# Constant operand rows of the first batch loaded in two parts, the second behind the first operand loads

## The chip, the cores and the metric

The kernel runs on one core of a Trainium2 chip. The metric is the time of the whole program on the device, in microseconds (us). Five engines work beside each other, each through its own queue in order: PE (TensorE, matrix products), DVE (VectorE), ACT (ScalarE), POOL (GpSimd) and SP (SyncE, which here issues DMAs and computes nothing). ACT and POOL issue DMAs too. A DMA's data are moved by the core's 16 DMA engines.

## The reference, cut to what matters

Input is `x` of shape (8, 512, 128): 8 batches of 512 tokens. Four sublayers follow each other, each with a residual and a layer norm:

```python
x = _layernorm(x + _L0_attn_ref(x, ...))   # 16 heads of 8, with a linear distance bias
x = _layernorm(x + _L0_ffn_ref(x, ...))    # gated, blockwise FP4 quantisation
x = _layernorm(x + _L1_attn_ref(x, ...))   # 16 heads of 8, no bias
x = _layernorm(x + _L1_ffn_ref(x, ...))    # two layers of windowed attention and GEGLU
```

The change lies in the first one:

```python
slopes = jnp.power(2.0, 8.0 * jnp.arange(0, -H, -1) / H)
q, k, v = heads of (x @ W_qkv.T + b_qkv)
scores = jnp.einsum('bhqd,bhkd->bhqk', q, k) / math.sqrt(Hd)
rel = jnp.abs(pos[None, :] - pos[:, None])
probs = jax.nn.softmax(scores - slopes * rel, axis=-1)
out = (probs @ v, heads joined) @ W_out.T + b_out
```

## The kernel before, in words

**Operands.** For one batch, the operand tiles `qs_[i]` and `ks_[i]` (i is the batch's parity) have 128 partitions, 8 pairs of heads and 512 tokens. The partitions are two halves of 64, j = 0 and 1, one for each head of a pair. Of a half, partitions 0 to 31 hold four groups of 8 rows: the head's 8 dimensions, split in a high and a low float32r part and put in the products that are wanted. Partitions 32 to 47 hold the constant rows `rowq` or `rowk`, the same for all pairs, from which the same matmul makes the greater part of the distance bias. Partition 63 holds -1 in `ks_` (row 16 of `rowk`) and, in `qs_`, the row maxima that are put there later. A scores matmul reads 63 or 64 partitions of one pair, so it needs the loaded rows and the constant rows of that pair.

**How the first batch gets there.** `constant_rows(0, held)` (line 1147, called in 1205) copies the constant rows from SBUF to SBUF, all 8 pairs, in six DMAs on SP: for each half one for row 63 of k, one for the 16 rows of q, one for the 16 rows of k. Then `attention` (line 252) is called. Its `plan` (line 392) makes the first batch's operands: `begin_x` transposes x, `begin_qk` (line 212) projects q, then k, lets POOL split them into `parts`, and writes these to DRAM (`far`, two DMAs each, one for each half). `load_qk` (line 232) reads them back in the order of rows that the tiles want, with eight DMAs of 8 partitions for each call:

```python
for part in (slice(0, 2), slice(2, 4), 1):
    load_qk(0, batch[0], 0, part, held)
    load_qk(0, batch[0], 1, part, held_a)
```

So pairs 0 and 1 come first, then 2 and 3, then 4 to 7; q on SP (`held`), k on ACT (`held_a`). Behind these on SP come, through `first_late` (line 1166), the constant rows of the second batch (`constant_rows(1, held)`), the x of batches 2 to 7 (`load_late`, line 103) and then the weights of the next sublayer.

**Steps.** Attention is a row of steps, 8 for each unit of two pairs (four units a batch). Step s of the scores takes pair `2 * g + i % 2` and the query block `i // 2`: steps 0 to 7 need pairs 0 and 1, steps 8 to 15 pairs 2 and 3, steps 16 to 31 pairs 4 to 7, and step 32 begins the second batch. In a step PE makes the scores of a block of 128 queries for both heads (`s_ps`), DVE takes their row maxima (`m`). PE's buffer `s_ps` is double. `LAG` = 16 steps later the same unit's transposed scores (`t_ps`) go through ACT's exponentials (`e`) to the product with v (`av`); `shift` (line 323) takes the maxima of a unit to row 63 of q with a POOL DMA. The second batch's operands are begun at steps 8 (`begin_x`), 10 and 12 (`begin_qk`).

**Order and waits.** Whatever goes through `held`, `held_a`, `Kept` or `keep_in_program_order` stays in the order of the program on its queue. The framework puts semaphore waits between tiles' writers and readers, by region. Its DMAs on SP and ACT share eight completion semaphores in turn, and a DMA is issued only when the one before it on the same semaphore has landed.

Of the kernel before, what the change touches and what calls it, by code (L numbers as in the profile page):

```python
# [9 lines left out]
F32 = mybir.dt.float32  # L10
# [9 lines left out]
B, S, D = 8, 512, 128  # L20
# [31 lines left out]
def body(ctx, tc, x, consts, rows, wa0, wa1, acols, bo, wf, wqkv, wo, w1, w2, cols, b2r, qs, ks, out):  # L52
# [26 lines left out]
    held, held_a = (lambda e: lambda **k: tc.keep_in_program_order(e.dma_start(**k)))(nc.sync), (  # L79
        lambda e: lambda **k: tc.keep_in_program_order(e.dma_start(**k))  # L80
    )(nc.scalar)
# [21 lines left out]
    def load_late():  # L103
        for b in range(2, B):
            held(out=xn[:, b * NT : (b + 1) * NT, :], in_=xv[:, b])
# [64 lines left out]
    def quantized_tokens(b, y, m, small):  # L170

        flat = lambda t: t[:, b * NT : (b + 1) * NT, :].rearrange("p c d -> p (c d)")
        return quantized(flat(xn), S, y, m, flat(xs), small)
# [75 lines left out]
        return begin_x, begin_qk, load_qk, begin_v  # L249


    def attention(li, alibi, qs_, ks_, va, batch, late=None, spare=None, alone=0):

# [4 lines left out]
        with ExitStack() as st:  # L260
# [9 lines left out]
            def with_bias(b):  # L270
                for c in range(NT):
                    pool_.tensor_tensor(xs[:, b * NT + c, :], xn[:, b * NT + c, :], crow, ALU.add)
# [119 lines left out]
            def plan():  # L392
                nonlocal work, crow
                const, work = pool("ac", 1), pool("aw", 2)
                dram = pool("ad", 2, space=bass.MemoryType.DRAM)
                begin_x, begin_qk, load_qk, begin_v = operand_steps(
                    li, qs_, ks_, va, mm, tr, bank, work, dram, qb[:, li : li + 1]
                )

                bvb = const.tile([P, P], F32, name="bvb")  # L400
                dve.tensor_copy(bvb, col[:, 3:4].broadcast_to([P, P]))
                crow = const.tile([P, P], F32, name="crow")
                nc.scalar.dma_start(out=crow, in_=bo[li].partition_broadcast(P))
                for n in range(B * G):
                    b, g = divmod(n, G)
                    s, z = n * NU, n * NU + LAG
                    later(z + 12, divide, units[n])
                    for blk in range(NT):
                        for part in range(2):
                            later(z + 2 * blk + 3 + part, values, units[n], blk, part)  # L410
                    if g == 0 and begun <= b + 1 < B:

                        early = max(s - 10, 8)
                        later(early, begin_x, b + 1, batch[b + 1])
                        later(early + 2, begin_qk, b + 1, batch[b + 1], 0)
                        later(early + 4, begin_qk, b + 1, batch[b + 1], 1)
                        for part in range(2):
                            for j in range(2):
                                later(max(s, 8) + 6 + 12 * part + 2 * j, load_qk, b + 1, batch[b + 1], j, part)
                        later(s + 20, begin_v, b + 1, batch[b + 1])  # L420
                        later(s + 20, with_bias, b + 1)
                    if g == 0:
                        later(s + 20 if b else alone, hold_o, batch[b])
                    if g == G - 1:
                        later(z + 15, end_o, batch[b])
                        later(z + 18, end_y, b, batch[b])
                if not begun:
                    begin_x(0, batch[0])
                    begin_qk(0, batch[0], 0, held)
                    begin_qk(0, batch[0], 1, held)  # L430
                    begin_v(0, batch[0])
                    for part in (slice(0, 2), slice(2, 4), 1):
                        load_qk(0, batch[0], 0, part, held)
                        load_qk(0, batch[0], 1, part, held_a)

                def bias_row():
                    ps = bank("c_ps")[:, 0:P]
                    mm(ps, lhsT=bvb, rhs=w[:, W_O : W_O + P], start=True, stop=True)
                    dve.tensor_tensor(crow, ps, crow, ALU.add)
                    for b in range(max(begun, 1)):  # L440
                        with_bias(b)

                later(alone + 4, bias_row)
                if late:
                    late()
                if spare:
                    spare(later, lambda b: (b * G + G - 1) * NU + LAG + 22, work, bank, mm, tr, p_s)

            for s in range(B * G * NU + LAG + 20):
                if s == alone:  # L450
                    plan()
                n, i = divmod(s, NU)
# [691 lines left out]

    with tc.tile_pool(name="ops", bufs=1) as ops:
        qs_, ks_ = ([at, ops.tile([P, 8, S], F32R, name=f"{n}1")] for n, at in (("q", q0), ("k", k0)))
        def constant_rows(i, start):
            for j in range(2):
                for t, at, src in ((ks_[i], 63, rowk[16:17]), (qs_[i], 32, rowq), (ks_[i], 32, rowk[0:16])):
                    n = src.shape[0]  # L1150
                    start(
                        out=t[64 * j + at : 64 * j + at + n].bitcast(F32),
                        in_=src.bitcast(F32).unsqueeze(1).broadcast_to([n, 8, S]),
                    )

        va = [va0, ops.tile([P, NT, 16, 32], F32, name="va1")]

        def filled(v):
            pool_.memset(v, 0.0)
            pool_.memset(v[:, :, :, 8:9], 1.0)  # L1160

        filled(va[0])
        wgu = ops.tile([P, 2, NI], F32, name="wgu")
        wd = ops.tile([P, 3, D], F32, name="wd")

        def first_late():
            dve.memset(qs_[1].bitcast(F32), 0.0)
            pool_.memset(ks_[1].bitcast(F32), 0.0)
            filled(va[1])
            constant_rows(1, held)  # L1170
            load_late()

        def first_spare(later, done, work, bank, mm, tr, p_s):
            temps = lambda: [work.tile([P, S], F32, tag=t, name=t, bufs=1) for t in ("qy", "qm")]
            later(64, load_weights)
            for j in range(3):
                quantize_weights(later, 28 + 11 * j, j, temps, work, bank, tr)

            def tokens(b):
                for i, f in zip((1, 4, 5, 6), quantized_tokens(b, *temps(), work)):  # L1180
                    later(done(b) + i, f)

            for b in range(B - 1):
                later(done(b), tokens, b)

            def turned():

                ps, h["xT"] = bank("xq_ps")[:, 0 : 2 * P], work.tile([P, S], F32, tag="qy", name="xqT", bufs=1)
                for t in range(2):
                    tr(ps[:, t * P : (t + 1) * P], xs[:, t, :], ident)  # L1190
                act_.copy(h["xT"][:, 0 : 2 * P], ps)

            def table():

                one = small.tile([P, 1], F32, tag="one", name="one", bufs=1)
                act_.activation(one, half[:, 0:1], AF.Silu)

            h, end = {}, done(B - 1) - 22 + 2 * NT
            later(end - 1, turned)
            later(end + 2, lambda: gates.append(gate(h["xT"], 0)))  # L1200
            later(end + 3, table)
            later(end + 5, lambda: gates.append(gate(h["xT"], 1)))

        second, gates = [], []
        constant_rows(0, held)
        psum = ExitStack()
        p_s, p_t, p_av = (
            psum.enter_context(tc.tile_pool(name=n, bufs=k, space=PSUM)) for n, k in (("as", 2), ("at", 3), ("aav", 1))
        )
        for _ in attention(0, True, qs_, ks_, va, [], first_late, first_spare):  # L1210
            pass
        nc.gpsimd.memset(rowq.bitcast(F32), 0.0)
        for i in range(2):
            for j in range(2):
                nc.sync.dma_start(
                    out=ks_[i][64 * j + 32 : 64 * j + 48].bitcast(F32),
                    in_=rowq.bitcast(F32).unsqueeze(1).broadcast_to([16, 8, S]),
                )
        last = ffn1()
        for _ in ffn0(qs_, ks_, va, second, gates, lambda: attention(1, False, qs_, ks_, va, second, spare=last[0], alone=16)):  # L1220
            pass
        psum.close()
# [98 lines left out]
```

## Time and profile before

| | us |
|---|---|
| median of 3 runs | 1742.46 |
| lowest and highest | 1741.09, 1747.34 |
| profiled execution, its own time | 1744.98 |
| span of the profiled execution | 1743.1 |
| PE busy in the span | 1637.8 (94%) |

The profile is one execution. Its times count from the start of the span. In its lists a line has the start, the length, the engine (a `q` behind it means the engine's queue, so an issue and no work of the engine), the operation and `out<-in` by the program's names; a length of several instructions (`x4`) goes from the first start to the last end. The length of a DMA in a queue is the time its issue took, not that of its data. In the chain of waits "DMA q<-far" is time until the landing of such a DMA. Waits are inferred from semaphore events. The granted clock is the share of full speed at which PE was let run.

### The profile page before, as it was taken

Reading aid. Unit: us, or ns where it says so; the run is one execution under the profiler, and the core shown is the slowest. Engines: PE = TensorE matmul, PEld = TensorE weight load, DVE = VectorE, ACT = ScalarE, POOL = GpSimd, SP = SyncE. Lnnn points to the kernel's source line nnn. Section 1 sums busy time; section 2 is a strip of 40 time slices with the busy share of each in tenths; the row PEclk is TensorE's granted clock in tenths of the full one; section 3 lists DMA queues with packets and bytes.
Section 4 is the critical chain, followed back from the end, with each engine's and each line's share of the span. In section 5 each row is a group of like instructions: output and inputs, shape, how many; then the busy total and the mean of one; then the engine's idle time right before and its main releaser. Section 6 shows DMA issues by size and latency. Waiting matters only on the chain.

```text
span 1743.1 us, 42097 instructions
## 1 busy us (share of the span) xinstructions
PE 1637.8 (94%) x16304; PEld 950.2 (55%) x16305; DVE 1381.6 (79%) x2209; ACT 1257.5 (72%) x2996; POOL 911.9 (52%) x974
## 2 busy tenths in 40 slices
PE   4999999999988789999999989999999999999995
PEld 2455555455546544444444446666766666666664
DVE  4688777878839888888888847788888888888873
ACT  1577777776764558878778867788887888888883
POOL 3223331332126741323222257888888888888873
PEclk7799999999999989999999999999999999999998
DMA  5735222321110234333323101111111111111110
GB/s 125 155 68 143 65 54 47 67 59 26 14 14 1 73 66 84 64 62 73 68 52 55 44 1 35 35 35 38 41 38 35 35 41 38 44 41 42 37 35 25
DMA packets 80777, 90.27 MB, mean 52 GB/s; under 512 B 46097, under 2 KB 58385, under 8 KB 76610
## 3 DMA queue, kind: packets, MB, share of 16 engines
q1 hardware_dynamic: 75504, 85.52, 23.2%
q8 instruction: 130, 2.13, 0.5%
q10 hardware_dynamic: 978, 1.52, 0.3%
q0 software_dynamic: 4096, 0.54, 0.3%
q14 instruction: 69, 0.57, 0.1%
HBM read 41.85 MB, written 18.87 MB: 35 GB/s over the span
## 4 chain that ended last, share of the span: by engine, by line
PE 77%; DVE 7%; ACT 6%; POOL 5%; issue 2%; DMA 2%; SPq 1%; DVEq 0%; POOLq 0%; ACTq 0%
PE av L258 15%; PE s_ps L258 12%; PE t_ps L258 9%; PE y_ps L645 5%; PE sp L645 4%; PE o_ps L645 3%; PE t_ps L645 3%; PE v_ps L645 3%; PE p_ps L645 2%; PE q_ps L645 2%; PE k_ps L645 2%; ACT e L48 2%; PE gp L645 2%; PE ap L645 2%; PE o_ps L259 2%
## 5 line engine op out<-in xcount | busy, mean ns | idle before, releaser
L48 DVE TENSOR_REDUCE m<-s_ps 128x2 f32<-128x1024 f32 x512 | 622.5, 1224 | 154.1 <-PE s_ps L258 148.9
L48 ACT ACTIVATE e<-t_ps 128x512 f32<-128x512 f32 x1024 | 556.3, 596 | 178.4 <-PE t_ps L258 170.1
L258 PE MATMUL av<-e,va 128*32 128x256 f32 x4096 | 328.1, 393 | 10.8 <-ACT avs L48 10.7
L258 PE MATMUL s_ps<-k,q 63*128 63x512 f32 x1024 | 265.3, 511 | 20.5 <-DMA q<-far 14.4
L48 POOL DMA_DIRECT2D q<-mt x128 | 68.9, 542 | 365.9 <-ACT mt L48 365.9
L258 PE MATMUL t_ps<-q,k 64*128 64x512 f32 x1024 | 248.1, 448 | 1.3 <-ACT e L48 1.3
L645 ACT ACTIVATE pw<-sp,m,was_v 128x128 f32<-128x128 f32 x512 | 227.6, 480 | 1.5 <-DVE m L645 1.0
L258 PEld LDWEIGHTS s_ps<-k,q 63*128 63x128 f32 x1024 | 99.8, 189 | 227.9 <-issue 151.3
L645 POOL TENSOR_TENSOR was_v<-was_v 128x16 f32<-128x16 f32 x64 | 187.6, 2931 | 5.3
L258 PEld LDWEIGHTS av<-e,va 128*32 128x32 f32 x4096 | 81.5, 108 | 100.5 <-issue 58.9
L258 PEld LDWEIGHTS t_ps<-q,k 64*128 64x128 f32 x1024 | 122.5, 189 | 22.7 <-ACT e L48 10.6
L645 POOL TENSOR_TENSOR pw<-pw,den 128x1024 f32<-128x1024 f32 x64 | 121.3, 1895 | 9.1 <-DVE den L645 9.1
L645 ACT ACTIVATION_READ_ACCUMULATOR pw<-sp,m,was_v 128x1 f32 x512 | 115.9, 226 | 0.0
L258 PEld LDWEIGHTS <-sel 64*128 64x128 bf16 x2048 | 67.3, 98 | 76.6 <-issue 53.3
L645 DVE TENSOR_REDUCE m<-sp 128x4 f32<-128x512 f32 x128 | 82.2, 683 | 21.9 <-PE sp L645 20.1
L48 POOL CAST parts<-x 128x512 fp32r<-128x512 f32 x32 | 19.5, 610 | 138.4 <-ACT x L48 138.4
L645 POOL TENSOR_TENSOR was_k<-was_k,was_q 128x512 f32<-128x512 f32 x64 | 88.0, 1376 | 6.1 <-DVE was_q L645 6.1
L645 ACT COPY v<-v_ps 128x512 f32<-128x512 f32 x64 | 37.6, 588 | 72.7 <-PE v_ps L645 72.7
L645 PEld LDWEIGHTS t_ps<-cst,was_k 128*128 128x128 f32 x512 | 59.7, 142 | 43.2 <-issue 22.4
L645 DVE COPY pT<-p_ps 128x512 f32<-128x512 f32 x128 | 79.8, 664 | 0.5 <-PE p_ps L645 0.5
L645 PEld LDWEIGHTS p_ps<-cst,pw 128*128 128x128 f32 x512 | 59.8, 141 | 33.0 <-issue 28.0
L645 DVE TENSOR_REDUCE was_v<-was_k 128x16 f32<-128x1024 f32 x64 | 77.0, 1204 | 0.0
(191 smaller groups left out, 3282.1 us busy)
## 6 DMA issues: line engine op xcount, KB each, us to landing
far<-parts SPq DMA_DIRECT2D x64, 256.0 KB
q<-far SPq DMA_DIRECT2D x248, 64.0 KB
k<-far SPq DMA_DIRECT2D x240, 64.0 KB
ve<-v SPq DMA_DIRECT2D x112, 128.0 KB
xn<-in_x SPq DMA_DIRECT2D x8, 256.0 KB
q<-mt POOLq DMA_DIRECT2D x128, 4.0 KB, 3.1
hn<-xs SPq DMA_DIRECT2D x16, 128.0 KB
hn<-xs SPq DMA_DIRECT2D x16, 112.0 KB
```

What stands on the lines that cost most here:

```text
L48: return lambda *a, **k: self.tc.keep_in_program_order(f(*a, **k))
L258: mm = lambda *a, **k: tc.keep_in_program_order(nc.tensor.matmul(*a, **k))
L259: tr = lambda *a, **k: tc.keep_in_program_order(nc.tensor.transpose(*a, **k))
L645: kept = lambda f: lambda *a, **k: tc.keep_in_program_order(f(*a, **k))
```

## The change

`constant_rows` gets a range of pairs. Before the first attention only pairs 0 and 1 are copied; the call for pairs 2 to 7 is handed to `attention` as `between` and made in `plan` after the loads of pairs 0 and 1. Both parts go through `held`, so the second part's six DMAs stand on SP behind q's eight loads of pairs 0 and 1 and ahead of q's loads of pairs 2 and 3. The second batch's call is unchanged.

```diff
-    def attention(li, alibi, qs_, ks_, va, batch, late=None, spare=None, alone=0):
+    def attention(li, alibi, qs_, ks_, va, batch, late=None, spare=None, alone=0, between=None):
...
                     for part in (slice(0, 2), slice(2, 4), 1):
                         load_qk(0, batch[0], 0, part, held)
                         load_qk(0, batch[0], 1, part, held_a)
+                        if between and part == slice(0, 2):
+                            between()
...
-        def constant_rows(i, start):
+        def constant_rows(i, start, pp=slice(0, 8)):
             for j in range(2):
                 for t, at, src in ((ks_[i], 63, rowk[16:17]), (qs_[i], 32, rowq), (ks_[i], 32, rowk[0:16])):
                     n = src.shape[0]
                     start(
-                        out=t[64 * j + at : 64 * j + at + n].bitcast(F32),
-                        in_=src.bitcast(F32).unsqueeze(1).broadcast_to([n, 8, S]),
+                        out=t[64 * j + at : 64 * j + at + n, pp].bitcast(F32),
+                        in_=src.bitcast(F32).unsqueeze(1).broadcast_to([n, pp.stop - pp.start, S]),
                     )
...
-        constant_rows(0, held)
+        constant_rows(0, held, slice(0, 2))
...
-        for _ in attention(0, True, qs_, ks_, va, [], first_late, first_spare):
+        for _ in attention(0, True, qs_, ks_, va, [], first_late, first_spare, between=lambda: constant_rows(0, held, slice(2, 8))):
```

## The prediction

> **What bounds the kernel now.** I read the page's parts 1 and 4 first, then the chain of waits over the first 42 us, then SyncE's own queue and the DMA queues there, then stage windows. The page says that TensorE sets the time once it runs:
>
> ```profile
> span 1743.1 us, 42097 instructions
> PE 1637.8 (94%) x16304; PEld 950.2 (55%) x16305; DVE 1381.6 (79%) x2209; ACT 1257.5 (72%) x2996; POOL 911.9 (52%) x974
> PE 77%; DVE 7%; ACT 6%; POOL 5%; issue 2%; DMA 2%; SPq 1%; DVEq 0%; POOLq 0%; ACTq 0%
> ```
>
> So this change can act in one place only: the start, where TensorE has no operands yet. The chain in order of time (start, length, what) is there:
>
> ```profile
> 13.53 1.55 POOL parts L48 x2
> 15.08 7.30 DMA far<-parts
> ...
> 22.44 2.93 DMA q<-far
> 25.39 2.45 DMA q<-far
> ...
> 28.16 2.07 DMA q<-far
> 30.24 0.90 PE s_ps L258 x4
> ...
> 39.66 0.93 PE s_ps L258 x3
> ```
>
> The operands are ready in SBUF at 14.80 (POOL), go out to DRAM (`far`), come back as `q` and `k`, and the first scores start at 30.24. From there VectorE's maxima pace the steps (nine of 1.21 to 1.23 us from 31.16 to 41), and step 8, the first to read pairs of heads 2 and 3, starts at 39.66.
>
> SyncE's queue, start, length and count:
>
> ```profile
> 7.47 0.84 SPq L79 DMA_DIRECT2D k<-rowk  x1
> 8.36 0.76 SPq L79 DMA_DIRECT2D q<-rowq  x1
> 9.16 2.54 SPq L79 DMA_DIRECT2D k<-rowk  x2
> 11.75 2.58 SPq L79 DMA_DIRECT2D q<-rowq  x1
> 14.38 0.60 SPq L79 DMA_DIRECT2D k<-rowk  x1
> 15.08 7.17 SPq L79 DMA_DIRECT2D far<-parts  x4
> 22.44 16.47 SPq L79 DMA_DIRECT2D q<-far  x24
> ```
>
> The issue of the six constant DMAs ends at 14.98, hardly later than the operands are ready; but their data are still moving. Windows (us, busy time of the five engines, granted clock, DMA share, GB/s):
>
> ```profile
> 15.00:20.00 5.00, 0.37 (x2) 0.07 (x1) 0.00 (x0) 0.59 (x1) 4.92 (x3) 0.92 0.94 102
> 20.00:24.00 4.00, 0.00 (x0) 0.00 (x0) 0.00 (x0) 0.00 (x0) 2.10 (x3) 0.50 0.88 246
> 24.00:28.00 4.00, 0.07 (x1) 0.10 (x1) 0.00 (x0) 0.00 (x0) 0.00 (x0) 0.50 0.42 131
> 53.00:67.00 14.00, 14.00 (x101) 8.86 (x104) 7.62 (x7) 6.14 (x12) 3.20 (x7) 0.51 0.94 245
> ```
>
> The constants are 4 x 262 KB and 2 x 16 KB, 1.08 MB (two halves j; 16 rows of q and of k and one of k, eight pairs, 2 KB each). At the 100 GB/s that the DMA view shows for 10 to 20 us they need 10.8 us. 0.05 MB moved before 9 us, 0.53 from 9 to 15 (88 GB/s), 0.51 from 15 to 20: they are out at about 20.2. Only then does `far` move, at 246 to 282 GB/s, and its first part has landed at 22.38, that is 2.2 us after its data could start.
>
> **The change, part by part.**
>
> *First part ahead of `far`.* The six DMAs stay six, a quarter the size: 0.27 MB, 2.7 us of data. Issue is 0.60 to 0.84 us each where the queue is not full, so 3.6 to 5.0 us: 11.1 to 12.5; data out by 13.5. That is over a microsecond ahead of 14.80, so it is hidden by the projections and POOL's splitting (1.27 us, until 14.80). The issue of `far` moves from 15.08 to 14.85: 0.2 us. From issue to data I take 1.0 us (bounds 0 and 1.4: the first constant is issued at 7.47, and in the DMA view the rate first jumps, to 102 GB/s, at 8.9). q's first load then goes at 14.85 + 1.0 + 2.2 = 18.05 instead of 22.44. k's halves are ready at 15.44 + 1.26 = 16.70; their `far` lands at 16.75 + 1.0 + 2.2 = 19.95, where k's first load went at 24.16 before. k is last, so step 0 gains **4.2 us**. Bounds: 5.2 with no delay to the data; 3.0 where the rest of the constants runs beside k's last four loads (2 KB packets of 0.31 us, one ahead of each: 4 x 0.31 = 1.2).
>
> *The rest behind the first loads.* This adds six DMAs on SyncE, 0.81 MB, 8.1 us of data at 100 GB/s. Queued behind them there: q's loads of pairs 2 and 3 (eight), then of 4 to 7, then batch 1's constants and the remaining inputs. ScalarE's queue of k loads is not passed, but shares the DMA engines. When do they start? In the trace the ninth load after `far` went 5.42 us after the first (27.86 against 22.44), held by earlier landings. So: 18.05 + 5.4 = 23.5 and 1.0 to the data; 24.5 + 8.1 = 32.6 out. q's loads of pairs 2 and 3 took 6.0 us from first issue (27.86) to last landing (33.87). Of that, one group of four (2.9 us, 22.44 to 25.39) can be issued before the constants are out: 35.7 if all of it overlaps, 38.6 if none does, 40.3 if the eight k packets of pairs 2 and 3 on each engine (0.215 us each) also come first. I take 37.5, between the first two, since the trace's loads always ran with four in flight.
>
> *What is late next.* Step 8 wants those pairs at 39.66 - 4.2 = 35.5. It stalls 37.5 - 35.5 = 2.0 us, and the net is **4.2 - 2.0 = 2.2 us**; bounds 4.2 (nothing late; 5.2 with the other bound) to -0.6 (landing at 40.3). Pairs 4 to 7 (q's last issue at 38.65 before, some 4 us later now) are due in step 16, at 52.73 before: covered by 8 us. ScalarE's last k issue (40.93 before) stands ahead of its copy of batch 1's x (42.11); k starts 4.2 earlier and meets 1.7 us of shared packets more, so it isn't later. Batch 1's constants, six inputs and its `far` (56.90) come up to 4 us later; its operands begin to return at 61.77 and are due in step 32, at 87.2. Covered.
>
> *The clock.* From 20 to 48 the granted clock is 0.50, and again from 53 to 67 (0.51) though TensorE is busy there without a gap. That stretch holds 14 us of work that would take some 7 at full clock, and its end may move by steps of 3.4 us (the grants in the record are multiples of it), each worth 1.7 us. I count nothing for it and keep 3.4 either way for the range. The Trainium skill (TensorE: Matmul & The Clock Gate, section on the HAM clock gate) has a free-running window of 3.4 us; by it a shift of the whole start moves these edges by chance. The trace's 14 busy microseconds at half clock are more than its one window.
>
> [...]
>
> **Sum.** Profiled execution: 1744.98 us for a span of 1743.1; less 2.2 is 1742.8. It stands 2.5 above the median of the three runs (1742.46, from 1741.09 to 1747.34), so by the median the forecast is **1740.3 us**. A measurement of this kernel tells about 0.5%, 8.7 us, from no change.
>
> **The rivals.**
>
> 1. *Half kept* (forecast): 1740.3; chance 0.45.
> 2. *All kept*: the loads of pairs 2 and 3 land by 35.5 because constants use DMA engines that the loads leave idle (share only 0.42 from 24 to 28). For it: that share. Against: 0.94 wherever constants run. 1742.46 - 4.2 = 1738.3; with the half clock ending four windows sooner, 6.8 more, 1731.5. Chance 0.22, of which 0.10 beyond 0.5%.
> 3. *Starved step 8* (slower): on SyncE the loads of pairs 2 and 3 are issued only as constants land, so both groups of four follow the last constant: 40.3 + 2.9 = 43.2 against 39.66, 3.5 us late, 1746.0. It decides from a landing past 39.66; past 0.5% only at 48.4, or with clock lost and pairs 4 to 7 late for step 16 too. For it: every q load of the trace waits for a landing. Against: k's queue is free of constants. Chance 0.23, of which 0.12 beyond 0.5%.
> 4. *Nothing moves*: `far` is slow by itself, not for the constants: 1742.5. Against: 102 GB/s turning into 246 at 20 us, after the constants' count of bytes. Chance 0.10.
>
> **Numbers.** Faster by over 0.5%: 0.10; within: 0.78; slower: 0.12. Low: 1738.3 less a clock gain of 3.4 and the runs' 1.4 below the median, 1733. High: 1746.0 and 3.4 of clock, 1749.4, so 1750.
>
> **What would show it.** Right: six constant issues done by 12.5, `far` issued at 14.9, q's first load near 18, first scores near 26, six more constant issues from 23 to 31 us, step 8 near 37.5 with a DMA wait ahead of it, and from step 16 on every row some 2 us earlier. Wrong: `far` landing later than 20; step 8 without a wait (rival 2) or after 39.66 (rival 3); or a difference that arises after 70 us, which none of these steps explains.

## The result, and the profile after

The changed kernel takes 1747.87 us (median of 22 runs) against 1741.61 us: ratio 1.0037, 95% interval 1.0027 to 1.0047, some 6.3 us slower (4.7 to 8.2). The forecast was 2.2 us faster. The time lies in the range that was given, the sign is wrong.

The start went as forecast. The first scores' maxima begin 4.3 us sooner than before, and then step 8 comes 5.3 us later. VectorE's timeline of the changed kernel (start, length, count of steps):

```profile
26.88 5.75 DVE L48 TENSOR_REDUCE m<-s_ps 128x2 f32<-128x1024 f32 x5 [13.62 <-PE s_ps L258]
...
32.98 3.49 DVE L48 TENSOR_REDUCE m<-s_ps 128x2 f32<-128x1024 f32 x3
46.27 1.23 DVE L48 TENSOR_REDUCE m<-s_ps 128x2 f32<-128x1024 f32 x1 [9.81 <-PE s_ps L258]
```

The same lines of the kernel before:

```profile
31.16 5.75 DVE L48 TENSOR_REDUCE m<-s_ps 128x2 f32<-128x1024 f32 x5 [17.60 <-PE s_ps L258]
...
41.01 1.23 DVE L48 TENSOR_REDUCE m<-s_ps 128x2 f32<-128x1024 f32 x1 [0.27 <-PE s_ps L258]
```

Now steps 0 to 7 end at 36.5, then VectorE is idle for 9.81 us. Before, steps 0 and 8 began 9.85 us apart; now the distance is 19.39. SyncE's queue shows where the loads of pairs 2 and 3 stand:

```profile
7.26 0.80 SPq L79 DMA_DIRECT2D k<-rowk  x1
...
10.91 0.59 SPq L79 DMA_DIRECT2D k<-rowk  x1
14.53 3.13 SPq L79 DMA_DIRECT2D far<-parts  x4
17.84 4.77 SPq L79 DMA_DIRECT2D q<-far  x8
23.81 0.84 SPq L79 DMA_DIRECT2D k<-rowk  x1
24.70 0.67 SPq L79 DMA_DIRECT2D q<-rowq  x1
26.16 3.93 SPq L79 DMA_DIRECT2D k<-rowk  x2
32.14 0.62 SPq L79 DMA_DIRECT2D q<-rowq  x1
33.15 0.59 SPq L79 DMA_DIRECT2D k<-rowk  x1
33.95 11.80 SPq L79 DMA_DIRECT2D q<-far  x16
```

The first part and `far` are where they were wanted: constants issued by 11.5, `far` at 14.53, q's first load at 17.84 instead of 22.44. But the second part's six issues are spread over ten microseconds, and q's loads of pairs 2 and 3 begin only at 33.95. Their eight went at 27.86 to 31.8 before. The chain of waits names the constants and loads in turn:

```profile
16.42 3.83 DMA far<-parts
...
27.41 4.71 DMA k<-far
...
32.14 6.00 DMA q<-rowq
...
38.16 4.93 DMA q<-far
...
45.35 0.29 PE s_ps L258 x2
```

What SyncE's queue waited for between its issues from 24 to 46 us (us in total, times, longest):

```profile
SPq L79 <- DMA q<-rowq: 4.2, 2, 2.5
SPq L79 <- DMA k<-far: 2.8, 4, 2.0
SPq L79 <- DMA k<-rowk: 2.4, 2, 1.7
SPq L79 <- DMA q<-far: 2.3, 4, 1.2
```

Two of these waits held up q's loads of pairs 2 and 3 themselves: the third went at 38.16, when a constant DMA had landed, the fifth at 40.45, when the last constant DMA had (1.6 and 1.7 us of waiting). ScalarE's queue, meanwhile, ran through all of k's 24 loads, those of pairs 4 to 7 too (from 30.85 on, by its single issues):

```profile
20.27 20.04 ACTq L80 DMA_DIRECT2D k<-far  x24
```

The DMA view of the stretch from 24 to 41 us counts what was moved (packets, MB, share of the engines' time; q1 is SyncE's queue, q10 ScalarE's):

```profile
DMA packets 788, 1.70 MB, mean 100 GB/s; under 512 B 232, under 2 KB 232, under 8 KB 732
...
q1 hardware_dynamic: 509, 0.90, 44.4%
q10 hardware_dynamic: 279, 0.80, 21.8%
```

Of the 1.70 MB, 0.81 are constants, and nearly half came from ScalarE's queue. All together moved 100 GB/s, as the constants alone did before. But the 16 engines were in use for only 66% of the time (44.4 + 21.8), against 94% with constants alone (from 15 to 20 us before) and 42% with loads alone (from 24 to 28 us before): 5.7 of the 17 us of engine time went unused.

### The profile page after: what moved, and what is told of

The parts are those of the page before. It is cut to its first block, busy times and chain, and to the rows that moved or that the text cites. A ratio compares the mean times of both kernels' runs of the same rounds, so it can differ in the third digit from the quotient of the medians.

```text
span 1743.5 us, 42098 instructions
## 1 busy us (share of the span) xinstructions
PE 1637.5 (94%) x16304; PEld 948.0 (54%) x16305; DVE 1381.9 (79%) x2209; ACT 1256.8 (72%) x2996; POOL 912.1 (52%) x974
## 4 chain that ended last, share of the span: by engine, by line
PE 76%; DVE 7%; ACT 6%; POOL 5%; DMA 3%; issue 2%; SPq 1%; ACTq 0%; DVEq 0%; POOLq 0%
PE av L258 15%; PE s_ps L258 12%; PE t_ps L258 9%; PE y_ps L647 5%; PE sp L647 4%; PE o_ps L647 3%; PE t_ps L647 3%; PE v_ps L647 3%; PE q_ps L647 2%; PE k_ps L647 2%; PE p_ps L647 2%; ACT e L48 2%; PE gp L647 2%; PE ap L647 2%; PE o_ps L259 2%
## 5 line engine op out<-in xcount | busy, mean ns | idle before, releaser
L258 PEld LDWEIGHTS t_ps<-q,k 64*128 64x128 f32 x1024 | 122.4, 189 | 23.0 <-ACT e L48 11.1
```

Source lines behind the costliest of these rows:

```text
L258: mm = lambda *a, **k: tc.keep_in_program_order(nc.tensor.matmul(*a, **k))
```

## The experiments

The theories as they stood: **A1**, SyncE loses its time by waiting, DMA after DMA, for landings in the eight shared semaphores; **A2**, the bytes of the second part, and whatever shares the DMA engines with them, stand ahead of the loads; **C**, the loss lies elsewhere, in the start's chance or the half-clock stretches. "Distance" below is from the start of step 0's maxima to that of step 8's: 9.85 before, 19.39 after.

**Second part left out.**

```diff
-between=lambda: constant_rows(0, held, slice(2, 8))
+between=lambda: None
```

> Leaves out the constant rows of pairs 2 to 7 of the first batch altogether (the bias of these heads is missing in batch 0). Theory A (the second part's DMAs, on SP, hold up q's loads of pairs 2 and 3, so step 8 starves): with the six DMAs gone step 8's maxima start as many us behind step 0's as before (9.85), so at 26.9 + 9.9 = 36.7 instead of 46.3, and the time is 4.3 us under before, about 1737. Rival C (the 6 us come from the half-clock stretches or from somewhere later): step 8 still moves, but the time stays at 1745 to 1748.

Measured:

```profile
28.30 5.75 DVE L48 TENSOR_REDUCE m<-s_ps 128x2 f32<-128x1024 f32 x5 [14.31 <-PE s_ps L258]
...
38.15 1.23 DVE L48 TENSOR_REDUCE m<-s_ps 128x2 f32<-128x1024 f32 x1 [0.27 <-PE s_ps L258]
```

Distance 9.85; 1737.83 us against 1741.32, ratio 0.9988 (0.9974 to 1.0002). The whole loss hangs on these six DMAs; C is out as its main cause. Step 0 itself came 1.4 us later in this run than in the changed kernel's first profile, which is why 38.15 isn't the 36.7 that was expected.

**A sixth of the bytes.**

```diff
-between=lambda: constant_rows(0, held, slice(2, 8))
+between=lambda: constant_rows(0, held, slice(2, 3))
```

> Six DMAs in the same place, but of pair 2 alone (0.13 MB instead of 0.81; the rows of pairs 3 to 7 are left out, so their bias is missing in batch 0). A2 (bytes): 6.7 us less data, step 8's maxima at 37 to 39. A1 (waits in turn): the six issues still each wait for a landing, some 2 us apart, so q's loads of pairs 2 and 3 still start after 30 and step 8 is at 40 to 44.

Measured, in VectorE's timeline:

```profile
27.46 5.75 DVE L48 TENSOR_REDUCE m<-s_ps 128x2 f32<-128x1024 f32 x5 [13.80 <-PE s_ps L258]
...
37.21 1.23 DVE L48 TENSOR_REDUCE m<-s_ps 128x2 f32<-128x1024 f32 x1 [0.16 <-PE s_ps L258]
```

Distance 9.75: six DMAs in the same place, with the same semaphores, cost step 8 nothing when they are small. A1 as the expectations price it, so much for each turn, falls. That leaves the bytes, and waits that grow with the bytes they wait for.

**The same bytes in twelve DMAs.**

```diff
-between=lambda: constant_rows(0, held, slice(2, 8))
+between=lambda: (constant_rows(0, held, slice(2, 5)), constant_rows(0, held, slice(5, 8)))
```

> The second part as twelve DMAs of three pairs instead of six of six: the same bytes in the same place, twice the turns in the shared semaphores. A2 (bytes): step 8's maxima at 45 to 47, as before this edit. A1 (waits in turn): six more waits of 1 to 2 us each, step 8 at 50 or later.

Measured:

```profile
27.80 5.75 DVE L48 TENSOR_REDUCE m<-s_ps 128x2 f32<-128x1024 f32 x5 [13.95 <-PE s_ps L258]
...
47.22 1.23 DVE L48 TENSOR_REDUCE m<-s_ps 128x2 f32<-128x1024 f32 x1 [9.84 <-PE s_ps L258]
```

Distance 19.42. With six DMAs it is 19.39 in one profile of the changed kernel and 18.43 in another (below), so a profile tells it to about 1 us. Within that, twice the DMAs cost nothing; six more waits of 1 to 2 us each, as A1 had it, would show.

**k's loads of pairs 4 to 7 put behind q's.**

```diff
-load_qk(0, batch[0], 1, part, held_a)
+load_qk(0, batch[0], 1, part, held if part == 1 else held_a)
```

> As the changed kernel, but k's eight loads of pairs 4 to 7 (0.52 MB, due in step 16 only) go on SP behind q's instead of on ACT. Theory A2, made sharper: step 8 is late because these loads, which run ahead on ACT's queue, share the DMA engines with the constants (8 packets of 8 KB at 0.6 us on each loaded engine, 4.8 us) and hold back q's loads of pairs 2 and 3. Then step 8's maxima come at 46.3 - 4.8 = 41 to 42, step 16 no later than 13 us behind that, and the time is some 4 us under the changed kernel, 1743 to 1744. Rival (the constants' bytes alone make the delay, the k loads don't matter): step 8 stays at 45 to 46, time 1746 to 1748.

Measured:

```profile
27.31 5.75 DVE L48 TENSOR_REDUCE m<-s_ps 128x2 f32<-128x1024 f32 x5 [13.96 <-PE s_ps L258]
...
42.51 1.23 DVE L48 TENSOR_REDUCE m<-s_ps 128x2 f32<-128x1024 f32 x1 [5.62 <-PE s_ps L258]
```

Distance 15.20, and 1744.18 us, ratio 1.0019 (1.0006 to 1.0033). Of the 9.54 us by which the distance grew (19.39 - 9.85), 4.2 go with loads that nobody wants before step 16 (3.2 by the second profile of the changed kernel). The edit takes these loads out of the DMA engines' way and, at once, out of the turns in the shared semaphores, so it doesn't tell which of the two costs the time. The other 5.3 go with the constants, but that their bytes alone cost it isn't shown. In this run SyncE's queue waited once for 4.9 us, until 32.02, for a load of k to land before it could issue the fourth constant DMA, and from 32 to 34 us the DMA engines were nearly idle (share 0.04, 6 GB/s):

```profile
SPq L79 <- DMA k<-far: 4.9, 1, 4.9
...
32.00:34.00 2.00, 2.00 (x14) 1.07 (x13) 1.85 (x3) 0.00 (x0) 0.66 (x2) 0.50 0.04 6
```

How the 5.3 us divide between bytes and such waits, no run shows.

**Second part from POOL's queue.**

```diff
-between=lambda: constant_rows(0, held, slice(2, 8))
+between=lambda: constant_rows(0, pool_.dma_start, slice(2, 8))
```

> Same second part, issued by POOL's queue, whose DMAs complete on semaphores of their own. Theory A1 (what hurts is the wait of SP for landings, DMA after DMA, in the eight semaphores shared with ACT): q's loads of pairs 2 and 3 go right behind those of pairs 0 and 1, constants land by 31 to 35, step 8's maxima at 37 to 39, time 1737 to 1740. Theory A2 (what hurts is the 0.81 MB of constants in the DMA engines, whoever issues them): q's loads share the engines with the same bytes, step 8 at 43 to 46, time 1744 to 1748.

Neither case came, since POOL had nothing ahead of these DMAs and issued them at once. POOL's queue:

```profile
16.43 0.79 POOL L48 DMA_DIRECT2D k<-rowk  x1
...
19.39 0.52 POOL L48 DMA_DIRECT2D k<-rowk  x1
```

They ran beside `far` and the first loads, and step 0 went from 26.88 to 34.98:

```profile
34.98 5.75 DVE L48 TENSOR_REDUCE m<-s_ps 128x2 f32<-128x1024 f32 x5 [21.71 <-PE s_ps L258]
...
44.94 1.23 DVE L48 TENSOR_REDUCE m<-s_ps 128x2 f32<-128x1024 f32 x1 [0.38 <-PE s_ps L258]
```

The 8.1 us are as much as 0.81 MB take at 100 GB/s, and the distance is back at 9.96. So the bytes cost the same from another queue with semaphores of its own; they only hit another load. This agrees with the Trainium skill (DMA: Bandwidth & Descriptors, section on issuing engines, which aren't separate DMA queues): DMAs from all engines run on the same 16 DMA engines and interleave. The time, 1741.93 us (ratio 1.0008, 0.9993 to 1.0022), is better than such a start should give; the last section says why.

**Three parts, each ahead of its step.**

```diff
-if between and part == slice(0, 2):
-    between()
+if between and part != 1:
+    between(slice(2, 4) if part == slice(0, 2) else slice(4, 8))
```

> Three parts: pairs 0 and 1 ahead of far, pairs 2 and 3 (0.27 MB, 2.7 us) behind the first loads, pairs 4 to 7 (0.54 MB, 5.4 us) behind the second loads. By A2 q's loads of pairs 2 and 3 meet 2.7 us of constants and little of k's later loads: step 0's maxima at 27 to 28, step 8's 10 to 11 later at 37 to 39; the loads of pairs 4 to 7 meet the rest, step 16 at 50 to 54. Time 1738 to 1741. By A1 (waits in turn) step 8 is at 41 or later, time 1743 or more.

Measured: 27.25 and 38.23, distance 10.98, as A2 has it (2.7 us of constants instead of 8.1). But 1743.25 us, ratio 1.0007 (0.9993 to 1.0021): over the 1738 to 1741 expected of A2, and 6 us over its own profiled execution, 1736.9. Of the ten runs two lie under 1737, the profiled one among them, and eight between 1741.4 and 1746.1. So a second profile was taken:

> The three-part kernel once more: its profiled execution (1736.9) was 6 us under its median (1743.25). If its loads really come in time, step 8's maxima are again 11 behind step 0's and step 16's 23, and the median's 6 us are lost later, at half-clock stretches. If the first profile was a lucky draw of the loads, step 8 or step 16 is several us later in this one.

Step 8 has the same distance (11.07), but step 16 came at 53.16 instead of 50.25. A load of q, behind the third part, landed only at 52.10, just ahead of step 16's scores. Another 3 us follow by step 24 (63.27 in the first profile, 69.17 in the second). The two profiles from 52 to 62 us, the first above:

```profile
52.00:62.00 10.00, 9.72 (x116) 5.39 (x114) 6.84 (x7) 7.47 (x15) 3.21 (x7) 1.00 0.98 197
...
52.00:62.00 10.00, 9.77 (x76) 5.94 (x76) 5.96 (x5) 4.81 (x10) 3.21 (x7) 0.51 1.04 120
```

TensorE had the full clock in the first and half of it (0.51) in the second. That makes 5.9 of the 6.5 us between the two spans (1735.1 and 1741.6). The second execution, 1743.38, is like the median, so the first profile was the lucky draw. Whether the later step 16 brought the half clock, or chance, isn't shown.

**Four pairs first.**

```diff
-constant_rows(0, held, slice(0, 2))
+constant_rows(0, held, slice(0, 4))
-if between and part == slice(0, 2):
+if between and part == slice(2, 4):
-between=lambda: constant_rows(0, held, slice(2, 8))
+between=lambda: constant_rows(0, held, slice(4, 8))
```

> First part of four pairs ahead of far (0.54 MB, 5.4 us of data at 100 GB/s, out at 14.5 to 16), second part of pairs 4 to 7 behind the loads of pairs 2 and 3, whose rows are due only in step 16. A1 and A2 alike: step 0's maxima at 27 to 28, step 8's 9.9 later at 37 to 38, step 16 12.9 behind that at 50 to 51 if pairs 4 to 7 have landed by then; time 1738 to 1739, better than both. By A1 the loads of pairs 4 to 7 may come after 51 and give back 0 to 3 us. C: no better than before.

Measured: 28.49 and 38.34 (distance 9.85), then step 16 at 53.70 where a start 2.67 us sooner than before should have given 51.3; it gives back 2.4 us. The expectation had put such a loss down to A1, so on this point A1 had it right, and waits in SyncE's queue stay a possible cause of it. 1737.47 us, ratio 0.998 (0.9967 to 0.9992): faster than both. The profiled execution was one of the two longest of the ten (1742.41), so its step 16, 0.2 us ahead of the kernel before, doesn't show where the median's 3.9 us come from.

**Four pairs first, the rest behind all loads.** As above, with `part == 1` for the condition.

> Four pairs ahead of far, the constants of pairs 4 to 7 behind all loads of the first batch (due in step 16). By A2 the order of bytes is then the order in which the steps want them: loads of pairs 2 and 3 by 33, of 4 to 7 by 41, constants by 46 to 47; no step waits, so step 0's maxima at 28 to 29, step 8's at 38, step 16's at 50 to 51. 3 to 4 us under before, 1737 to 1738.5, and no slower than the kernel with the rest behind the loads of pairs 2 and 3. Rival: the constants land after 50 and step 16 gives back 2 to 3 us, 1739 to 1741.

Measured:

```profile
28.75 5.75 DVE L48 TENSOR_REDUCE m<-s_ps 128x2 f32<-128x1024 f32 x5 [14.56 <-PE s_ps L258]
...
38.61 1.23 DVE L48 TENSOR_REDUCE m<-s_ps 128x2 f32<-128x1024 f32 x1 [0.27 <-PE s_ps L258]
...
51.13 2.36 DVE L48 TENSOR_REDUCE m<-s_ps 128x2 f32<-128x1024 f32 x2 [0.83 <-PE s_ps L258]
```

VectorE is idle for 0.27 us ahead of step 8 and 0.83 ahead of step 16. But the slack is used up: constants were expected by 46 to 47, and the chain of waits has a landing of constant rows at 50.51 right ahead of step 16's scores:

```profile
47.18 3.33 DMA k<-rowk
...
50.55 0.24 PE s_ps L258 x2
```

1737.11 us against 1740.49, ratio 0.998 (0.9969 to 0.9991). This is the idea of the change with the bytes in the order in which the steps want them.

**Second profiles of both kernels.**

> The changed kernel once more, for a second profile. A2 puts the whole loss before step 16, as a fixed matter of DMA order: step 8's maxima 19.4 behind step 0's again (within 0.3), and 5 us behind the kernel before at step 16; whatever else its span differs by arises at the edges of half-clock stretches (0 to 5 us). Rival C (the first profile's start was a rare draw): step 8 less than 18 or more than 21 behind step 0.

> The kernel before once more. A2: step 8's maxima 9.85 behind step 0's (within 0.3); its span differs from the first profile's 1743.1 only by the half-clock stretches and the first loads, and is likely 1736 to 1742, since the first profile was 2.5 us over the median.

Measured for the changed kernel:

```profile
27.56 5.75 DVE L48 TENSOR_REDUCE m<-s_ps 128x2 f32<-128x1024 f32 x5 [13.97 <-PE s_ps L258]
...
45.99 1.23 DVE L48 TENSOR_REDUCE m<-s_ps 128x2 f32<-128x1024 f32 x1 [8.85 <-PE s_ps L258]
```

Distance 18.43, under the expected 19.1 to 19.7, and 9.86 for the kernel before, as expected. At step 16 the changed kernel is 4.5 us behind in the second pair of profiles (57.59 against 53.07) and 4.9 in the first (58.84 against 53.94). The spans differ by 0.4 us in the first pair (1743.5 against 1743.1) and by 7.8 in the second (1746.8 against 1738.9).

## Why the prediction was wrong, point by point

- **First part hidden, `far` free: right.** The six issues ended at 11.5 (forecast 11.1 to 12.5), `far` went at 14.53 (14.85), q's first load at 17.84 (18.05), k's at 20.27 (19.95).
- **Start gain of 4.2 us: right.** 4.28 in the first profiles, 4.10 in the second (31.66 less 27.56).
- **Start of the constants: right.** 23.81 against 23.5.
- **Landing of pairs 2 and 3 at 37.5: here lies the step that failed.** Their scores began at 45.35, 7.9 us later. The term is the constants' data, "24.5 + 8.1 = 32.6 out": the last constant DMA landed near 40.4, 7.8 us later than that. From there to step 8's scores it took 4.9 us, as much as the forecast had (37.5 - 32.6), in part by luck, for only two of q's loads were issued ahead of the constants' landings where the forecast had four. The 8.1 us let the constants move without a break at 100 GB/s, as they do in the kernel before, where no loads run beside them. In the changed kernel SyncE's queue had to wait between the six issues, and in the 17 us from 24 to 41 the DMA engines worked for SyncE's queue for 7.5 us (44.4%), for ScalarE's k loads for 3.7 (21.8%), and stood idle for 5.7 (an average over the 16). For the k loads the prediction had 1.7 us, those of pairs 2 and 3, in its bound alone. It left out those of pairs 4 to 7, 0.52 MB, which ScalarE's queue issued while SyncE's was held up; with them put behind q's the distance was 3.2 to 4.2 us shorter. The rest, some 4 us, is shown to hang on the constants (the run without them). How it divides between shared engines and waits in turn stays open.
- **Net of 2.2 us gained: wrong**, since 4.28 gained less 9.54 lost is 5.26 lost.
- **Rival 3, starved step 8: right in its place and its sign**, with 43.2 for the landing where the trace has about 45. Its mechanism, loads of q "issued only as constants land", is in the trace: the third and the fifth of the eight waited for a constant DMA's landing, at 38.16 and 40.45. The runs with one pair and with twelve DMAs add that such turns cost nothing when what they wait for is small, and no more when there are twice as many for the same bytes. Its counterargument, that k's queue is free of constants, was a part of the cause.
- **Rival 2** spoke of DMA engines that the loads leave idle. There was idle time, a third of the stretch from 24 to 41 us, but q's loads stood in SyncE's queue and could not use it: the first went at 33.95, the third only at 38.16.
- **Later dues covered: right for the changed kernel.** No later step waits for operands: from step 24 to past 500 us the first two profiles run 3.5 to 3.6 us apart.
- **The clock: counted at nothing, kept in the range.** Behind step 16 the two kernels' distance changes by more than a few tenths only where one of them is at half clock while the other isn't. First pair: 4.9 at step 16, 3.5 from step 24, 3.8 until 1000 us, 0.4 from 1140. Second pair: 4.5 at step 16, 4.8 until 610 us, 9.6 by 690, 8.0 from 1100. The start's loss at step 16, 4.5 and 4.9 us, lies at the low end of the median's interval (4.7 to 8.2). That the change brings more half clock near 610 to 650 us is possible (24 and 27 us of it there in the changed kernel's two profiles, 17 in both of the kernel before), but two profiles each don't show it; it stays open.

## What to carry to other kernels

Splitting a transfer is worth what its first part frees, less what its second part then stands in front of. Sum the bytes of every queue that feeds the same DMA engines up to each step's due time: here a queue that wasn't held up ran ahead with loads that were due later. A rate read where one kind of transfer runs alone (100 GB/s, 94% of the engines) need not hold where issues wait for landings (66%). Cut the parts by the order in which the steps want them, and put what is due last behind everything, on all queues.

## What the runs showed of the hardware that was not expected

The time behind the last output differed with what POOL issued. In the trace the drain of POOL's queue at the end took 10.77 or 10.78 us in the twelve profiles of kernels whose POOL issued 128 DMAs, and 1.39 us in the kernel that issued six more there; its span ended 7 us sooner for it, which is why it lost so little. A last run tried this on the best version, with six later weight loads issued by POOL:

```diff
-held(out=wo_s, in_=wo.rearrange("l (c p) d -> p l c d", p=P))
+pool_.dma_start(out=wo_s, in_=wo.rearrange("l (c p) d -> p l c d", p=P))
...
```

> As the kernel with four pairs first and the rest behind all loads, and six later weight loads (of step 64) issued by POOL instead of SP, as a trial of something seen beside the question: the one kernel with six more DMAs on POOL ended 7 us sooner behind its last output, with a final POOL drain of 1.39 us where every other profile has 10.77 or 10.78. If that hangs on the number of DMAs that POOL issues (134 instead of 128), the drain is 1.4 us here too and the time is 1729 to 1731. If it hung on something else in that kernel, the drain stays at 10.8 and the time at 1736 to 1739, or worse where POOL's issues hold up its layer norms at step 64.

The drain was 1.39 us again, so it goes with the six further DMAs in both kernels that have them. But the kernel took 1746.09 us, ratio 1.0025 (1.0011 to 1.0038): in the window behind these loads TensorE was busy for 12.00 of 22 us, where the best version has 21.55. The chain of waits shows what TensorE lacked: the small DMA that brings the row maxima into q (`q<-mt`), issued by POOL right behind the weights, took 16.26 us to land, where the median of all 128 is 3.1, and TensorE waited 10.0 us for it.

```profile
144.96 16.26 DMA q<-mt
...
PE t_ps L259 <- DMA q<-mt: 10.0, 1, 10.0
...
150.00:172.00 22.00, 12.00 (x115) 5.65 (x117) 7.11 (x6) 6.63 (x14) 1.05 (x2) 0.69 0.28 79
```

Six other DMAs of little weight were not tried, and why the drain differs is not known.
